# Head of a two-block attention kernel in another order, bias vectors moved into the MLP, and loop steps spread otherwise

## The chip, the cores and the metric

The kernel runs on one core of one Trainium2 chip. The metric is the device time of one execution in microseconds (us). All data are float32.

## The reference, cut to what matters

The input `x` has shape (2, 512, 32, 32). Two blocks follow each other.

```python
# block 0: deformable attention, 8 groups of 64 channels, 64 sampled keys per group
xn  = bn(x)
q   = gconv1x1(xn, qw)
off = tanh(einsum(gelu(depthwise6x6_stride4(q) + off_dw_b), off_pw_w)) * 4
vgrid = normalised(grid + off)                   # 64 key positions per group
kv  = bilinear_sample(xn, vgrid);  k, v = gconv1x1(kv, kw), gconv1x1(kv, vw)
pos = grid_q - vgrid                             # 1024 queries x 64 keys x 2
b   = sign(pos) * log1p(abs(pos))
b   = relu(b @ cpb_w1 + cpb_b1)                  # 2 -> 128
b   = relu(b @ cpb_w2 + cpb_b2)                  # 128 -> 128
b   = b @ cpb_w3 + cpb_b3                        # 128 -> 1
x   = x + out_w @ (softmax(q k / 8 + b) v) + out_b
x   = x + mlp_w2 @ gelu(mlp_w1 @ bn(x) + mlp_b1) + mlp_b2
# block 1: full attention over the 1024 positions, 512 channels
q, k, v = x Wq' + bq, x Wk' + bk, x Wv' + bv
x = x + (softmax(q k' / sqrt(512)) v) Wp' + bp
```

The position bias is the heavy part: its 128-to-128 layer runs for 2 x 8 groups x 1024 queries x 64 keys.

## The kernel before, in words

**Head.** The kernel first computes what is needed before its main loop. `chain(0)` (L251) normalises one 128-channel tile of `x` (L260), projects it to `q` on TensorE (PE, L266) with four copies out of PSUM (L271), runs the 36 taps of the depthwise convolution on VectorE (DVE, L303 and L305), GELU, a small projection (`po`, L345), tanh, and the positions of the keys with `sign * log1p` (L365 to L390). It writes the result to a DRAM buffer `fdr` through four DMAs on the queue of SyncE (SP), L392. `rank` and `arrange` (L208, L227) sort the hidden channels of the bias network by the sign of the last weight and permute its weights (`cw2`, `sc`). `weights(0)` and `weights(1)` (L518) multiply pairs of 512x512 matrices of block 1 on PE (`psg`, L524): Wq with Wk, and Wv with Wp. `vectors` (L534) does the same for the biases bq and bv: matmuls `psu` (L539) and `put` (L548) and the vector `ub` of block 1.

Each of these is a Python generator. The order in the head is the order in which lines 560 to 579 advance them, and `tc.issue_after` pins some pieces behind a given instruction. Around these pins the Tile layer orders instructions itself, engine by engine; each engine then runs its own list strictly in order.

**Loop.** `NS` = 256 steps `s`, each for four keys of one group. `load_tables` broadcasts a slice of `fdr` to all partitions (L592), `st_tables` makes tables `ta` and `tb` for 16 keys, that is every fourth step (L602, L609). `st_layer1(s + 2)` adds them on DVE with a saturating add into `h1` (L621, three buffers), `st_layer2(s)` is 64 matmul records on PE (L638) with four evictions on ScalarE (ACT, L645 and L647), `st_sum` joins them on DVE (L655), two accumulating DMAs of GpSimd (POOL) and one DMA of SP fold them, and every fourth step `st_layer3` (L703) adds to the logits.

Two background generators are spread over the steps. `bg` is `later()` (L480): the chains 1 to 4 and `sample` (keys and values), one `yield` piece per step. In chain 1 (one 128-channel tile) and chains 2 to 4 (two tiles each) the convolution taps run on ACT (L313), `TAPS[ci]` taps per piece, and DVE reduces them (L328). `tails` holds `softmax_steps` (L711) of a finished group, one piece per step:

```python
            if tails:
                with tc.issue_after(evicted[s][s % 4 == 0]):
                    if next(tails[0], 0) is not None:
                        tails.pop(0)
```

**After the loop.** `project` (L878) multiplies the attention output by `out_w` as seven Strassen-like products (L884) for each image, taken by DVE (L892, L123) with three PSUM buffers; `normalise` (L922) and `spread` prepare the MLP. Eight units of the MLP (L937) and block 1 (L1056, L1154) follow. Weights come over SP's queue (`load_unit`, L861).

Of the kernel before, what the change touches and what calls it, by code (L numbers as in the profile page):

```python
# [14 lines left out]
P = 128  # L15
# [11 lines left out]
TAPS = [36, 12, 4, 3, 3]  # L27
# [7 lines left out]
    ("bq", 4), ("bv", 4), ("bp", 4), ("dwb", 1), ("cb1", 1), ("cb3", 1),  # L35
# [11 lines left out]
def conv_seq_kernel(ctx: ExitStack, tc: tile.TileContext, x, xt, kst, pst, cst, vec, wsm, outw, w1, w2, wl, out):  # L47
# [16 lines left out]
    for i, g in enumerate(("bn1g", "bn2g")):  # L64
        nc.gpsimd.tensor_scalar(
            bns[:, 4 * i : 4 * i + 4], vs[:, VOFF[g] : VOFF[g] + 4], INV_BN, None, ALU.mult
        )
# [73 lines left out]
    with tc.tile_pool(name="lp", bufs=2) as lp:  # L141
# [20 lines left out]
        nc.gpsimd.memset(prod, 0.0)  # L162
# [12 lines left out]
        nc.scalar.dma_start(out=pz[:, 0:413], in_=pst)  # L175
        nc.scalar.dma_start(out=ws[:, 1024:1408], in_=wsm[:, 1536:1920])
        nc.scalar.dma_start(out=ident, in_=kst)
        nc.scalar.dma_start(out=cs, in_=cst)
# [6 lines left out]
        xn0 = load(0, 0)  # L185
        nc.scalar.dma_start(out=ws[:, P:1024], in_=wsm[:, P:1024])
# [20 lines left out]
        perm, place = pw_[:, 256:384], pw_[:, 384:512]  # L207
        def rank():  # L208
            nc.gpsimd.memset(one, 1.0)
            nc.gpsimd.tensor_scalar(po_, wb[:, 0:1], 0.0, None, ALU.is_ge)  # L210
            ps = flat("rank")
            nc.tensor.matmul(ps[:, 0:1], tri, po_, start=True, stop=True)
            nc.tensor.matmul(ps[:, 512:513], one, po_, start=True, stop=True)
            nc.scalar.copy(rn, ps.rearrange("p (h n) -> p h n", h=2)[:, :, 0])
            r_, n_ = rn[:, 0:1], rn[:, 1:2]
            nc.gpsimd.tensor_scalar(pc, chan, n_, r_, ALU.add, ALU.subtract)
            nc.gpsimd.tensor_scalar(dc, pc, r_, po_, ALU.subtract, ALU.mult)
            nc.gpsimd.tensor_tensor(pc, pc, dc, ALU.subtract)
            nc.vector.tensor_scalar(k16, four, n_, 4.0, ALU.is_le, ALU.mult)
            nc.vector.tensor_reduce(t4, k16, AX.X, ALU.add)  # L220
            free, bound = ([t.rearrange("p (a b l) -> p b a l", a=2, b=2)[:, i] for t in (place, crow)] for i in (0, 1))
            nc.vector.tensor_scalar(bound[0], bound[1], t4, 64.0, ALU.is_ge, ALU.mult)
            nc.vector.tensor_tensor(bound[0], bound[0], bound[1], ALU.add)
            nc.vector.tensor_scalar(free[0], free[1], t4, None, ALU.add)
            nc.vector.tensor_scalar(perm, place, pc, None, ALU.is_equal)

        def arrange():  # L227
            ps = flat("perm")
            nc.tensor.matmul(ps[:, 0:P], w2t, perm, start=True, stop=True)
            for z in range(4):  # L230
                for u in range(4):
                    nc.tensor.matmul(
                        ps[32 * u : 32 * u + 32, 512 + 2 * z : 514 + 2 * z], perm[:, 32 * z : 32 * z + 32], wb,
                        start=True, stop=True,
                    )
            nc.scalar.copy(cw2, ps[:, 0:P])
            nc.scalar.copy(
                sc[:, 0:8].rearrange("p (a z) -> p z a", a=2), ps[:, 512:520].rearrange("p (z a) -> p z a", a=2)
# [7 lines left out]
            nc.gpsimd.tensor_scalar(w3u[:, 28:32], mask[:, 8:12], sc[:, 8:9], None, ALU.mult)  # L246

# [3 lines left out]
        def chain(ci):  # L251
# [3 lines left out]
            for i in range(K):  # L255
                k = k0 + i
                if i == 0:
                    xn = xn0 if ci == 0 else load(b, k)
                    yield
# [10 lines left out]
                for f_, h_, f, h in QUADS:  # L270
                    nc.scalar.copy(  # L271
                        qa[f_, b, k, h * 512 : (h + 1) * 512], ps[h_, f * 512 : (f + 1) * 512]
                    )
                if i + 1 < K:
                    xn = load(b, k + 1)
                yield
# [64 lines left out]
            ps = flat("po")  # L341
            with tc.issue_after(marks[0]) if ci == 0 else nullcontext():
                for i in range(3):
                    for f in range(2):
                        nc.tensor.matmul(  # L345
                            ps[:, f * 512 + i * n // 2 : f * 512 + (i + 1) * n // 2],
                            pw[i][64 * f : 64 * f + 64, :],
                            gof[64 * f : 64 * f + 64].rearrange("p k j -> p (k j)"), start=True, stop=True,
                        )
# [4 lines left out]
            for f in range(2):  # L354
                nc.scalar.activation(
                    th.rearrange("p i (f k) j -> p f i (k j)", f=2)[:, f],
                    ps[:, f * 512 : f * 512 + 3 * n // 2].rearrange("p (i m) -> p i m", i=3), AF.Tanh,
                )
            if ci == 0:

                nc.scalar.activation(hb[:, 9:10], thf[:, 3 * n - 1 : 3 * n], AF.Ln, bias=1.0, scale=0.0)
            if ci > 0:
                yield
            for i in range(3):
                nc.vector.scalar_tensor_tensor(  # L365
                    th[:, i], th[:, i], 4.0, jg[:, i].unsqueeze(1).to_broadcast([P, 2 * K, J]),
                    ALU.mult, ALU.add,
                )
            nc.vector.tensor_scalar(thf, thf, 2.0 / 7.0, -1.0, ALU.mult, ALU.add)
# [7 lines left out]
            if ci > 0:  # L377
                yield
            nc.vector.tensor_scalar(u, ab, 1.0, None, ALU.add)
# [5 lines left out]
            nc.vector.reciprocal(u, u)  # L385
            nc.vector.tensor_tensor(er, er, u, ALU.mult)
# [4 lines left out]
            for c in range(4):  # L391
                nc.sync.dma_start(  # L392
                    out=fdr[ci][:, c, :, :].rearrange("g p j -> p g j"),
                    in_=ab.rearrange("p (g c j) -> p g c j", c=4, j=KT)[:, :, c, :],
                )
# [111 lines left out]
        with tc.issue_after(nc.cur_bb.bb.instructions[-1]):  # L507
            nc.sync.dma_start(out=wv, in_=wsm[:, 1024:1536])
            nc.sync.dma_start(out=ow_s, in_=outw)
        gs = lp.tile([P, 2, NCH, C], F32, tag="h1", name="gs", bufs=3)  # L510
        bz = ph.tile([P, 2 * NCH, 32], F32, tag="xnt", name="bz")
        nc.gpsimd.memset(bz, 0.0)
        for i, bn in enumerate(("bq", "bv")):
            nc.gpsimd.tensor_copy(
                bz[:, i * NCH : (i + 1) * NCH, 0], vs[:, VOFF[bn] : VOFF[bn] + NCH]
            )

        def weights(i):  # L518
            ps = [flat("psg") for _ in range(2)]
            for o in range(NCH):  # L520
                if o == NCH - 1:
                    yield
                for k in range(NCH):
                    nc.tensor.matmul(  # L524
                        ps[k // 2][:, k % 2 * 512 : k % 2 * 512 + 512], wls[i][:, 0, o, k * P : (k + 1) * P],
                        wls[i][:, 1, o, :], start=(o == 0), stop=(o == NCH - 1),
                    )
            for k2 in range(2):
# [4 lines left out]

        def vectors():  # L534
            ps = flat("psu")
            rows = ph.tile([P, 2, C], F32, tag="wt", name="rows")
            for i in range(2):
                for o in range(NCH):
                    nc.tensor.matmul(  # L539
                        ps[32 * o : 32 * o + 32, 512 * i : 512 * i + 512], bz[:, i * NCH + o, :],  # L540
                        wls[i][:, 1, o, :], start=True, stop=True,
                    )
            nc.scalar.copy(rows.rearrange("p i c -> p (i c)"), ps)
            yield
            ps = flat("put")
            for i in range(2):
                for k in range(NCH):
                    nc.tensor.matmul(  # L548
                        ps[:, 512 * i + k : 512 * i + k + 1], rows[:, i, k * P : (k + 1) * P], ones,
                        start=True, stop=True,  # L550
                    )
            nc.scalar.copy(ub, ps.rearrange("p (i c) -> p i c", i=2)[:, :, 0:NCH])
            nc.gpsimd.tensor_tensor(
                ub[:, 1, :], ub[:, 1, :], vs[:, VOFF["bp"] : VOFF["bp"] + NCH], ALU.add
            )

        def newest(engine):
            return next(i for i in reversed(nc.cur_bb.bb.instructions) if i.engine == engine)

        marks = []  # L560
        head, g, n, v = chain(0), weights(0), weights(1), vectors()
        next(head)
        next(head)
        rank()
        next(head)
        next(g)
        marks.append(newest(mybir.EngineType.PE))
        next(head)

        with tc.issue_after(newest(mybir.EngineType.PE)):  # L570
            next(g, None)
        for _ in head:
            pass
        arrange()
        next(v)
        next(n)
        with tc.issue_after(newest(mybir.EngineType.PE)):
            next(v, None)
# [19 lines left out]
        def st_tables(c):  # L598
# [3 lines left out]
            nc.scalar.activation(  # L602
                ta.rearrange("p j x -> p x j"), fb[:, 0], AF.Identity, bias=col("cb1"), scale=col("w1x")
            )
# [167 lines left out]
        for s in range(NS):  # L772
# [37 lines left out]
            if tails:  # L810
# [28 lines left out]
    nc.gpsimd.tensor_tensor(uc, ub[:, 0, 0:2], ub[:, 0, 2:4], ALU.add)  # L839
# [16 lines left out]
    with ExitStack() as top, tc.tile_pool(name="wp", bufs=2) as wp:  # L856
# [171 lines left out]
        for i, (b, p) in enumerate(units):  # L1028
            if 0 < i < len(units) - 1:
# [6 lines left out]
            layer1(p, wa, xb, hm)  # L1036
            if p == NU - 1 and b == 0:
# [4 lines left out]
            if p == NU - 1 and b == 0:  # L1042
                spread([xb[:, j] for j in range(7)])

# [212 lines left out]
def _layout(np, inputs):  # L1257
# [7 lines left out]
    def twice(v):  # L1265
# [6 lines left out]
        "mb2": cols(L0["mlp_b2"]), "bq": cols(L1["bq"]), "bv": cols(L1["bv"]), "bp": cols(L1["bp"]),  # L1272
# [29 lines left out]
    def quarters(w):  # L1302
# [15 lines left out]
        "wl": wl,  # L1318
    }
# [20 lines left out]
```

## Time and profile before

| What | Value |
|---|---|
| Times of three runs | 2689.32, 2689.59, 2691.59 us (median 2689.59) |
| Profiled execution | 2690.77 us, span of its instructions 2688.9 us |
| Granted clock of TensorE | 0.998 |
| Busy in the span | PE 2664.8 us (99%), DVE 2244.6 (83%), ACT 1689.0 (63%), POOL 575.3 (21%) |
| First L638 matmul (loop begins) | 46.60 us |
| First L937 matmul (MLP begins) | 1996.00 us |

"Busy" is the share of the span in which an engine ran an instruction. A row of the timeline has the start, the length, the engine, the line, the operation with its tiles, and in brackets how long the engine sat idle before it and what it waited for. PEld is the weight load of PE, which overlaps its matmuls; SPq and POOLq are the queues that issue DMAs.

### The profile page before, as it was taken

What the parts mean: (1) busy time and instruction counts of PE and PEld (TensorE: products, weight loads), DVE (VectorE), ACT (ScalarE), POOL (GpSimd) and SP (SyncE); (2) the same over time, 40 slices, a digit from 0 to 9 for tenths busy, and PEclk for the clock granted to TensorE, in tenths of its full rate; (3) what the DMA queues carried; (4) which work ended last, traced back from release to release, by engine and by line L of the source; (5) the groups of instructions that cost most, each with busy time, mean ns of one, the idle gap of its engine ahead of it and who ended that gap; (6) DMA issues with size and microseconds to landing.
All of it is one profiled execution on the core that took longest, in us unless ns stands there. A gap on an engine that the chain in (4) does not pass through costs nothing.

```text
span 2688.9 us, 46981 instructions
## 1 busy us (share of the span) xinstructions
PE 2664.8 (99%) x19628; PEld 955.2 (36%) x19628; DVE 2244.6 (83%) x1337; ACT 1689.0 (63%) x2191; POOL 575.3 (21%) x617
## 2 busy tenths in 40 slices
PE   9999999999999999999999999999999999999999
PEld 3323323232333323233333333333344444446455
DVE  5999999999999999999999999999765484466354
ACT  4787798789878788877777777777621131114041
POOL 1222222222222222222222222222243222000000
PEclk9999999999999999999999999999999999999999
DMA  5667776677666676666676776766631110000000
GB/s 186 146 147 148 154 148 138 139 159 154 141 148 144 150 149 145 139 147 142 148 155 138 148 151 145 147 149 142 134 122 47 47 47 32 16 16 0 31 1 31
DMA packets 95219, 314.05 MB, mean 117 GB/s; under 512 B 17184, under 2 KB 19872, under 8 KB 92320
## 3 DMA queue, kind: packets, MB, share of 16 engines
q0 software_dynamic: 57168, 201.88, 40.4%
q1 hardware_dynamic: 36832, 108.02, 11.2%
q8 instruction: 155, 2.54, 0.4%
q10 hardware_dynamic: 1008, 1.15, 0.1%
q14 instruction: 56, 0.46, 0.0%
HBM read 71.67 MB, written 6.55 MB: 29 GB/s over the span
## 4 chain that ended last, share of the span: by engine, by line
PE 85%; DVE 6%; issue 4%; ACT 2%; DMA 2%; SPq 0%; POOL 0%; DVEq 0%; POOLq 0%; ACTq 0%
PE ps L638 54%; PE sw L937 14%; PE sw L1056 9%; DVE h L621 3%; PE sw L1154 2%; PE sim L703 2%; PE psg L524 1%; PE sw L884 1%; DVE ub L655 1%; DMA ua<-uo 1%; DVE uo L655 1%; DMA ua<-ua 0%; ACT prod L313 0%; DVE ua L655 0%; ACT rx L645 0%
## 5 line engine op out<-in xcount | busy, mean ns | idle before, releaser
L638 PE MATMUL ps<-h,cw 128*32 128x512 f32 x16384 | 1786.6, 593 | 12.3 <-ACT rx L645 10.7
L621 DVE CUSTOM_DVE_ANT_1 h<-ta,tb 128x4096 f32<-128x4096 f32 (+1 forms) x257 | 1131.3, 4402 | 47.0 <-PE ps L638 42.0
L638 PEld LDWEIGHTS ps<-h,cw 128*32 128x32 f32 x16384 | 533.9, 110 | 1231.7 <-issue 1151.7
L645 ACT ACTIVATE rx<-ps,sc 128x1024 f32<-128x1024 f32 x512 | 568.3, 1110 | 175.0 <-PE ps L638 165.5
L647 ACT ACTIVATE ub<-ps,sc 128x1024 f32<-128x1024 f32 x256 | 308.0, 1203 | 96.4 <-PE ps L638 96.2
L655 DVE SCALAR_TENSOR_TENSOR ub<-rx,sc,ub 128x1024 f32<-128x1024 f32 x256 | 326.5, 1275 | 5.7 <-ACT ub L647 5.5
L657 POOL DMA_DIRECT2D ua<-ub x128 | 115.1, 899 | 723.6 <-DVE ub L655 692.3
L937 PE MATMUL sw<-xb,w1t 128*128 128x512 f32 x448 | 193.7, 592 | 1.3 <-DVE xs L123 1.3
L657 POOL DMA_DIRECT2D uo<-ub x127 | 119.3, 939 | 348.8 <-DVE ub L655 289.0
L937 PE MATMUL sw<-hm,w2t 128*128 128x512 f32 x448 | 193.6, 592 | 0.0
L647 ACT ACTIVATE ua<-ps,sc 128x1024 f32<-128x1024 f32 x128 | 154.1, 1204 | 58.5 <-PE ps L638 58.3
L674 POOL DMA_DIRECT2D ua<-uo x126 | 109.7, 870 | 365.2 <-DMA ua<-uo 355.5
L647 ACT ACTIVATE uo<-ps,sc 128x1024 f32<-128x1024 f32 x128 | 154.1, 1204 | 42.0 <-PE ps L638 38.8
L655 DVE SCALAR_TENSOR_TENSOR ua<-rx,sc,ua 128x1024 f32<-128x1024 f32 x128 | 163.5, 1277 | 12.5 <-ACT ua L647 12.5
L655 DVE SCALAR_TENSOR_TENSOR uo<-rx,sc,uo 128x1024 f32<-128x1024 f32 x128 | 163.5, 1277 | 11.8 <-ACT uo L647 11.8
L123 DVE TENSOR_TENSOR hm<-hm,sw 128x1024 f32<-128x1024 f32 x56 | 67.5, 1220 | 110.8 <-PE sw L937 110.6
L669 POOL DMA_DIRECT2D ua<-ua x126 | 154.8, 1229 | 2.6 <-DMA ua<-ub 1.5
L937 PEld LDWEIGHTS sw<-xb,w1t 128*128 128x128 f32 x448 | 85.1, 190 | 108.8 <-issue 105.0
L946 ACT ACTIVATE hm<-hm,vs 128x512 f32<-128x512 f32 x64 | 42.6, 714 | 129.0 <-DVE hm L123 129.0
L937 PEld LDWEIGHTS sw<-hm,w2t 128*128 128x128 f32 x448 | 85.2, 190 | 107.1 <-issue 106.4
L123 DVE TENSOR_TENSOR xs<-xs,sw 128x1024 f32<-128x1024 f32 (+1 forms) x48 | 55.5, 1170 | 72.2 <-PE sw L1056 36.0
L1056 PE MATMUL sw<-aT,vt 128*128 128x512 f32 x224 | 96.7, 593 | 0.3 <-ACT aT L1136 0.3
(237 smaller groups left out, 1798.7 us busy)
## 6 DMA issues: line engine op xcount, KB each, us to landing
ua<-ub POOLq DMA_DIRECT2D x128, 512.0 KB, 4.8
uo<-ub POOLq DMA_DIRECT2D x127, 512.0 KB, 5.4
fb<-fdr SPq DMA_DIRECT2D x64, 512.0 KB, 5.1
ua<-ua POOLq DMA_DIRECT2D x126, 256.0 KB, 6.4
ua<-uo SPq DMA_DIRECT2D x126, 256.0 KB, 2.8
ua<-uo POOLq DMA_DIRECT2D x126, 256.0 KB, 3.8
w1t<-in_w SPq DMA_DIRECT2D x8, 1024.0 KB, 4.8
w2t<-in_w SPq DMA_DIRECT2D x8, 1024.0 KB, 4.8
```

The lines of the kernel that those rows point to most:

```text
L123: nc.vector.tensor_tensor(out, a, b_, op)
L621: nc.vector._custom_dve(TENSOR_ADD_SAT, out=h1[:, y : y + step].rearrange("p y t x -> p (y t x)"), in0=a.unsqueeze(1).to_broadcast([P, ste ...
L638: nc.tensor.matmul(ps[32 * q : 32 * q + 32, h, :], cw2[:, 32 * z : 32 * z + 32], h1[:, 16 * h : 16 * h + 16, q, :], start=True, stop=True,)
L645: nc.scalar.activation(o, ps, AF.Relu, bias=sc[:, 4 + z : 5 + z])
L647: nc.scalar.activation(o, ps, AF.Relu, bias=sc[:, 4 + z : 5 + z], scale=sc[:, z : z + 1])
L655: nc.vector.scalar_tensor_tensor(r[1], r[0], sc[:, z : z + 1], r[1], ALU.mult, ALU.add)
L657: nc.gpsimd.dma_start(out=sums[s][1], in_=sums[s][3], accum_op=ALU.add)
L669: nc.gpsimd.dma_start(out=lanes(s, 0), in_=lanes(s, 1), accum_op=ALU.add)
L674: nc.gpsimd.dma_start(out=lanes(s, 1), in_=lanes(s + 1, 0), accum_op=ALU.add)
L703: nc.tensor.matmul(sims[gi][q : q + 32, :], w_, t[:, h, :], start=(i == 0 and f == 0), stop=(i == NSL // 4 - 1 and m == len(parts[e]) - 1),)
L937: nc.tensor.matmul(ps[:, m, :], w[:, a, k, m * P : (m + 1) * P], x[:, b_, k, :], start=(k == 0), stop=(k == 1),)
L1056: nc.tensor.matmul(ps[:, m, :], w[:, a, k, c + m * P : c + (m + 1) * P], x[b_][:, k, :], start=(k == 0), stop=(k == nk - 1),)
```

## The change

The change has four parts.

1. **Head.** `vectors` is dropped. The normalisation scales are computed on DVE, three loads move from ACT's queue to POOL's, the load of the later q and k weights moves to the end of SP's list. `rank`, `order` (split off from it) and `arrange` use small PSUM tiles of the pool `simp` and other places in the order: the first matmuls of `weights(0)` now come before `rank`. Half of the copies of chain 0 go to DVE. The Ln table is loaded without waiting for tanh, x and y of the keys are placed after the write to `fdr`, and `u = ab + 1` moves from DVE to ACT. The four writes of each chain to `fdr` become one. The first table is made in two pieces.
2. **Chain pieces.** `TAPS` of chain 1 goes from 12 to 6 taps per piece; two `yield`s per chain go away; the next chain's `x` tile is loaded when the previous one has been projected.
3. **Softmax pieces.** No softmax piece in steps with `s % 4 == 0`, but for the last 16 steps.
4. **Bias vectors in the MLP.** For each of the eight units, SP loads a 128x512 slice of weights (`wr`, one buffer) and DVE multiplies it by the broadcast bias row (`br`, one buffer) and sums along the row into `ub`. In the built program the eight DVE instructions (L1032 of the changed kernel) stand among the last ones of `project` and the first ones of the MLP.

```diff
-TAPS = [36, 12, 4, 3, 3]
+TAPS = [36, 6, 4, 3, 3]
...
     for i, g in enumerate(("bn1g", "bn2g")):
-        nc.gpsimd.tensor_scalar(
+        nc.vector.tensor_scalar(
...
-        nc.scalar.dma_start(out=pz[:, 0:413], in_=pst)
         nc.scalar.dma_start(out=ws[:, 1024:1408], in_=wsm[:, 1536:1920])
-        nc.scalar.dma_start(out=ident, in_=kst)
-        nc.scalar.dma_start(out=cs, in_=cst)
+        nc.gpsimd.dma_start(out=cs, in_=cst)
+        nc.gpsimd.dma_start(out=pz[:, 0:413], in_=pst)
+        nc.gpsimd.dma_start(out=ident, in_=kst)
...
-        nc.scalar.dma_start(out=ws[:, P:1024], in_=wsm[:, P:1024])
...
                 if i == 0:
-                    xn = xn0 if ci == 0 else load(b, k)
-                    yield
+                    xn = xn0.pop()
...
                 for f_, h_, f, h in QUADS:
-                    nc.scalar.copy(
-                        qa[f_, b, k, h * 512 : (h + 1) * 512], ps[h_, f * 512 : (f + 1) * 512]
-                    )
+                    copy = nc.vector.tensor_copy if ci == 0 and h == 1 else nc.scalar.copy
+                    copy(qa[f_, b, k, h * 512 : (h + 1) * 512], ps[h_, f * 512 : (f + 1) * 512])
...
-                nc.scalar.activation(hb[:, 9:10], thf[:, 3 * n - 1 : 3 * n], AF.Ln, bias=1.0, scale=0.0)
+                with tc.issue_after(newest(mybir.EngineType.Activation)):
+                    nc.scalar.activation(hb[:, 9:10], ones, AF.Ln)
...
+            place_keys(2 if ci == 0 else 0, 3)
...
             nc.scalar.activation(ab, pos, AF.Abs)
-            if ci > 0:
-                yield
-            nc.vector.tensor_scalar(u, ab, 1.0, None, ALU.add)
+            nc.scalar.activation(u, ab, AF.Identity, bias=1.0)
...
-            nc.vector.reciprocal(u, u)
-            nc.vector.tensor_tensor(er, er, u, ALU.mult)
+            rc = acc.rearrange("p a k y x -> p (a k y x)")[0:64, 0:n]
+            nc.vector.reciprocal(rc, u)
+            nc.vector.tensor_tensor(er, er, rc, ALU.mult)
...
-            for c in range(4):
-                nc.sync.dma_start(
-                    out=fdr[ci][:, c, :, :].rearrange("g p j -> p g j"),
-                    in_=ab.rearrange("p (g c j) -> p g c j", c=4, j=KT)[:, :, c, :],
-                )
+            nc.sync.dma_start(
+                out=fdr[ci].rearrange("g c p j -> p (g c) j"), in_=ab.rearrange("p (g j) -> p g j", j=KT)
+            )
+            if ci == 0:
+                place_keys(0, 2)
...
+            nc.sync.dma_start(out=ws[:, P:1024], in_=wsm[:, P:1024])
...
-        head, g, n, v = chain(0), weights(0), weights(1), vectors()
-        next(head)
-        next(head)
-        rank()
+        head, g, n = chain(0), weights(0), weights(1)
         next(head)
         next(g)
-        marks.append(newest(mybir.EngineType.PE))
+        with tc.issue_after(newest(PE)):
+            rank()
         next(head)
-
-        with tc.issue_after(newest(mybir.EngineType.PE)):
-            next(g, None)
+        with tc.issue_after(newest(PE)):
+            next(g)
+        marks.append(newest(PE))
+        next(head)
+        with tc.issue_after(newest(PE)):
+            next(g)
+        order()
         for _ in head:
             pass
-        arrange()
-        next(v)
-        next(n)
-        with tc.issue_after(newest(mybir.EngineType.PE)):
-            next(v, None)
+        with tc.issue_after(newest(mybir.EngineType.Activation)):
+            next(g, None)
+        with tc.issue_after(newest(PE)):
+            arrange()
+        with tc.issue_after(newest(PE)):
+            next(n)
         next(n, None)
...
-            if tails:
+            if tails and (s % 4 or s >= NS - NSL):
...
         for i, (b, p) in enumerate(units):
+
+            j, k = divmod(i, NCH)
+            if k == 0:
+                br = cp.tile([P, C], F32, tag="kz", name="br")
+                nc.sync.dma_start(out=br, in_=brow[j].partition_broadcast(P))
+            wr = f_pool.tile([P, C], F32, tag="ss", name="wr")
+            nc.sync.dma_start(out=wr, in_=wlt[:, i])
...
             layer1(p, wa, xb, hm)
+            nc.vector.scalar_tensor_tensor(
+                wr, wr, 1.0, br, ALU.mult, ALU.mult, accum_out=ub[:, j, k : k + 1]
+            )
```

## The prediction

> **What bounds the kernel now.** I read first the page's busy times and costliest groups:
>
> ```profile
> PE 2664.8 (99%) x19628; PEld 955.2 (36%) x19628; DVE 2244.6 (83%) x1337; ACT 1689.0 (63%) x2191; POOL 575.3 (21%) x617
> L638 PE MATMUL ps<-h,cw 128*32 128x512 f32 x16384 | 1786.6, 593 | 12.3 <-ACT rx L645 10.7
> ```
>
> PE is busy 99%. So only three things can change the time: PE work that goes or comes, PE's idle gaps (2688.9 - 2664.8 = 24.1 us), and time in which PE runs slowly. In the timeline I then looked where these lie. The start:
>
> ```profile
> 6.26 1.24 ACT L260 ACTIVATE xn<-xn,vs,bns 128x1024 f32<-128x1024 f32 x1 [3.60 <-DMA ws<-in_wsm]
> 10.17 0.59 PE L212 MATMUL rank<-pwork,pz 128*128 128x1 f32 x2 [1.53 <-POOL pwork L210]
> 12.89 0.34 PEld L524 LDWEIGHTS psg<-wl_s 128*128 128x128 f32 x1 [0.52 <-issue]
> 13.75 0.34 PEld L524 LDWEIGHTS psg<-wl_s 128*128 128x128 f32 x1 [0.52 <-issue]
> 17.57 0.19 PEld L524 LDWEIGHTS psg<-wl_s 128*128 128x128 f32 x1 [0.24 <-issue]
> 18.00 0.19 PEld L524 LDWEIGHTS psg<-wl_s 128*128 128x128 f32 x1 [0.24 <-issue]
> 29.04 1.92 PE L539 MATMUL psu<-wl_s,bz 128*32 128x512 f32 x16
> 41.29 1.84 PE L548 MATMUL put<-ones,rows 128*128 128x1 f32 x16
> 41.66 4.49 DVE L621 CUSTOM_DVE_ANT_1 h<-ta,tb 128x2048 f32<-128x2048 f32 x2 [0.81 <-ACT ta L602]
> 46.60 0.16 PEld L638 LDWEIGHTS ps<-h,cw 128*32 128x32 f32 x8 [0.76 <-ACT gs L529]
> ```
>
> Between 1.56 and 46.60 us PE is the chain. It waits for the first normalisation, then for `rank`, and the weight products `psg` start slowly: 0.86 us from record to record (12.89, 13.75) until 16.28, then 0.43 (17.57, 18.00). The first `h1` is whole at 41.66 + 4.49 = 46.15, 0.45 us before PE asks.
>
> In the loop a plain step takes 6.87 us (64 records at 0.43 us, four at a time). Larger gaps are few. Windows give PE's idle time: 1.4 us from 46.6 to 352, 4.8 from 352 to 506.5, 6.1 from there to 1940, 2.8 from 1940 to 1996. Those that the change touches:
>
> ```profile
> 153.85 3.60 ACT L313 ACTIVATE prod<-qa,vs 128x49 f32<-128x49 f32 x12
> 161.59 3.69 ACT L313 ACTIVATE prod<-qa,vs 128x56 f32<-128x56 f32 x12
> ...
> 493.04 6.00 SPq L392 DMA_DIRECT2D fdr<-fe  x4
> 506.47 1.07 PE L638 MATMUL ps<-h,cw 128*32 128x512 f32 x8 [3.00 <-ACT rx L645]
> 508.64 0.22 PEld L638 LDWEIGHTS ps<-h,cw 128*32 128x32 f32 x4 [0.64 <-issue]
> 509.50 0.22 PEld L638 LDWEIGHTS ps<-h,cw 128*32 128x32 f32 x4 [0.64 <-issue]
> ...
> 1972.09 2.34 DVE L123 TENSOR_TENSOR xs<-xs,sw 128x1024 f32<-128x1024 f32 x2
> 1975.21 1.23 DVE L111 TENSOR_TENSOR xb<-xb 128x1024 f32<-128x1024 f32 x1 [0.78 <-ACT xb L927]
> 1994.72 1.22 DVE L123 TENSOR_TENSOR xs<-xs,sw 128x1024 f32<-128x1024 f32 x1 [0.68 <-PE sw L884]
> 1996.00 24.30 PE L937 MATMUL sw<-xb,w1t 128*128 128x512 f32 x56 [1.31 <-DVE xs L123]
> ```
>
> Twelve taps at once (3.6 us) delay ACT's evictions at 157 and 165: 1.4 us of PE idle. Chain 2's table write holds SP for 6.00 us, so the next table lands at 503.6, ACT waits 4.1 us in front of its evictions, PE 3.0, and then runs four records at 0.85 instead of 0.43. From 1958 to 1996 DVE, not PE, sets the pace: `project` has three PSUM buffers, each freed by DVE, which idles 3 us there.
>
> **The head, step by step.** ACT's list loses three loads; `vs` has landed at 4.70 and `xn` at 4.5, so the normalisation starts at about 5.25 instead of 6.26, and the projection follows the warm-up matmuls at 6.55 without a gap. The first four `psg` matmuls (8 records) follow at once: their operands land at 5.3 and 6.5. PE was at full pace at 7.55 (the projection took 1.09 us) and became slow after the idle time from 8.64; with no idle time it stays fast. So: 7.5 + 8 x 0.43 = 10.95; `rank` 0.87 gives 11.8; nine more matmuls (18 records) 7.7: 19.5; `po` 0.81: 20.3; the last three 2.6: 23.0 with the change-over; `perm` 0.59: 23.6; `weights(1)` 32 records, 13.7: **37.3 us** instead of 46.6. In that, 3.7 us are the two bias stages (1.92 + 1.84), 2.6 us six slow records, the rest gaps and waits.
>
> The tables must keep up. GELU's input is ready by 17.7: DVE starts the taps at about 9.0 (copies shared, two of 0.58 us each) and needs 36 x 0.225 = 8.1 plus 0.6 for sums. Tanh ends at 21.0. Before, DVE waited 1.0 us for the Ln dummy, the logarithm waited for a copy, and the reciprocal for the logarithm: 25.58 to 31.82, 6.2 us. Now: five small DVE steps 1.2, Abs and add on ACT 0.9, then 0.94 + 4 x 0.3: ready at 25.3. The write landed at 37.0 before, behind the `xnt` load (36.8) and in the traffic of the `gdr` write (35.5); `xnt` is now loaded long before, `gdr` starts at 25.5. I take 4.5 us for the one write (median of the four 4.3), so 29.8; `fb` 3.3: 33.1; table 0.4; two halves of `h1` 4.5: whole at 38.1. PE needs the second half 0.86 after its start, at 38.2. Bounds: landing in 3.5 us (no effect) or in 6.5 (2 us later). I take a start of 37.8: **-8.8 us** (-6.5 to -9.3). Moving three loads to POOL costs three issues of about 0.85 (the row of `gdr`: 0.81), before POOL has other work; `rank` needs `pz` at 10.95, five us after issue at most 9: hidden, and a late `pz` would cost PE its own delay, 0 to 2.
>
> **The loop.** Six taps are 1.8 us, and 1.8 + 4.6 (four evictions) fits into 6.87: **-1.4** (0 to -1.8). With one `yield` less in front and three pieces more in chain 1, chain 2 writes at step 57 instead of 58, with its table due at 60 as before. So the write leaves about 7.5 us earlier, the table is not late, and the 3.0 us and four slow records (4 x 0.38) go: **-4.5** (0 to -4.7). What is late next: `sample` reuses the tile `fe` two steps behind the write, and ACT must wait until the write has been read. Before chain 4 this wait cost ACT 2.4 us at 1151 and PE 1.9. The merged write moves the same 64-byte rows (1024 of them; the four landed 6.8 us after the first issue at 1144.8). For chains 2 and 3 I add **+1.0** (0 to +4). Gaps at 359, 662 and 774 follow steps with tables, and softmax pieces leave such steps; but DVE is 100% busy in those windows (352 to 506: 152 of 154.5), so I count nothing: what ACT no longer delays, DVE does. At the end four softmax copies (1.05 us) now stand ahead of the last eviction, which had 0.28 us of slack: **+0.8**.
>
> **The bias in the MLP.** Eight DVE instructions on 128x512, taken as 0.7 us (the 0.74 of L892). `wr` has one buffer, so each load waits for the instruction before, and in the built order five stand in `project`, where the products that free PSUM queue behind them. A lone 256 KB load: 1 MB of `w2t` lands 5.0 us after its issue, of which 2.6 at the 400 GB/s seen in the head, leaving 2.4 + 0.65 = 3.1. The second instruction then ends at 77.85 (1977.85) where DVE went on at 75.21, less later waits for ACT; the third is covered by 11 us of other work; the fourth waits 0.6; the fifth waits for `br` and `wr` behind the fourth. Walked through, the last `xs` sum ends at 1999.2 instead of 1995.94: **+3.3** (+1.5 with 2.0 us loads, +9 with the 5.3 of the `xs` row). The three in the first MLP unit stand where DVE idles 2.2 us per product: nothing. The gap in front of the MLP grows to over 3 us, and the trace showed slow records after 3.0 (at 506) and not after 1.9 (at 1152): **+1.2** (0 to 1.7).
>
> The Trainium skill, "DMA: Bandwidth & Descriptors" ("Anatomy of one DMA - SWDGE (gpsimd) path"), fits about 2.0 us plus bytes over 436 KB/us, which for 256 KB is 2.6 us; with that figure, an estimate from the page, the term would be +1.9 instead of +3.3. The same page ("SWDGE vs HWDGE vs iDMA") gives POOL's path the slower setup, which speaks against moving three loads there; no row here shows these loads on POOL.
>
> **Sum.** -8.8 - 1.4 - 4.5 + 1.0 + 0.8 + 3.3 + 1.2 = -8.4. On the profiled execution's own 2690.77 that is 2682.4; it lies 1.2 above the median of 2689.59, from which the sum gives **2681.2 us**. About 0.2%, 5.4 us, is what a measurement of this kernel can tell from no change: faster is below 2684.2.
>
> **Rivals.** (a) *The loop gives nothing back*: DVE is the limit wherever ACT's stalls go, and the gap at 506 returns as a wait for `fe`. For it: DVE's 152 of 154.5 us. Against: at 503 DVE had `h1` ready some 4 us ahead. Then -8.8 + 1.0 + 0.8 + 4.5 = -2.5: 2687, no change. 18%. (b) *Slower: the serial `wr` loads hold DVE's queue in front of the MLP*. Three round trips (second, fourth, fifth) lie open. With landing time L the term is 3.3 + 3 (L - 3.1), and it must exceed 12.9 + 5.4 - 1.7 = 16.6 to make the kernel slower: L over 7.5 us. The longest 512 KB table load in the loop took 7.8, but the queues at 1974 are empty (no DMA traffic from 1963.5 on). At 8 us: +18, sum +6.8, 2696. With small errors elsewhere 14%. (c) *The head moves less because the tables, not PE, set the loop's start*: with the write as late as bounded, -6.5: 2683.5, still faster; part of my case.
>
> **Numbers.** My case and (c) 68%. All best bounds together give about -15 (2674); the range reaches up to rival (a) with two more bad bounds: 2674 to 2692. It leaves out (b) and a few per cent.
>
> **Right or wrong.** In the profile after: the first L627 record near 37.8 (wrong above 40); `psg` records 0.43 apart from the first; no PE gap of 3 us near 495; no twelve-tap group; DVE rows of L1032 that wait for `wr` 1 to 2.5 us in `project`; the first L925 matmul 6 to 10 us earlier than 1996.0. A wait for `wr` of 5 us or more, or a start of the loop after 42, would make the forecast wrong.

## The result, and the profile after

| | us |
|---|---|
| Before, median of ten runs | 2689.95 (2689.32 to 2691.97) |
| Changed, median of ten runs | 2683.65 (2681.93 to 2688.11) |
| Ratio, 95% interval | 0.9979 (0.9971 to 0.9987) |
| Profiled execution, time and span: before | 2690.77 and 2688.9 |
| Profiled execution, time and span: changed | 2688.11 and 2686.3 |

The change makes the kernel faster by 6.3 us in the medians, 0.21% by the ratio in the table; forecast were 8.4 us and 2681.2 us. The profile of the changed kernel happens to be that of its slowest run: it is only 2.6 us shorter than the one of before. Eleven later runs of the changed kernel gave a median of 2685.33 us; over all 21 it is 2684.45, and that figure the experiments below are set against. Where an experiment gives a ratio to the kernel before, that kernel was run beside it (median 2690.19 us in 15 runs for e1 to e4, 2690.86 in 21 runs for the others).

From the page of the changed kernel, the busy times and the costliest group:

```profile
PE 2663.3 (99%) x19596; PEld 960.0 (36%) x19596; DVE 2249.2 (84%) x1353; ACT 1688.3 (63%) x2193; POOL 576.9 (21%) x615
L627 PE MATMUL ps<-h,cw 128*32 128x512 f32 x16384 | 1789.6, 593 | 11.5 <-DVE kv L475 8.6
```

PE still waits little. But the last column has changed: before, 10.7 of 12.3 us of the waits of this group were put down to ACT's evictions (`rx`), now 8.6 of 11.5 us are put down to `kv`, four small DVE instructions of `sample` that no step of the forecast had priced.

The head, in selected rows of the changed kernel's timeline (start, length, engine, line, tiles, then the idle time before and its releaser):

```profile
7.75 3.70 PE L533 MATMUL psg<-wl_s 128*128 128x512 f32 x8
25.30 0.70 SPq L405 DMA_DIRECT2D fdr<-fe  x1
30.98 5.47 SPq L579 DMA_DIRECT2D fb<-fdr  x2
35.37 8.83 DVE L610 CUSTOM_DVE_ANT_1 h<-ta,tb 128x2048 f32<-128x2048 f32 x3 [0.23 <-ACT ta L590]
37.71 1.06 PE L627 MATMUL ps<-h,cw 128*32 128x512 f32 x8
39.91 5.36 PE L627 MATMUL ps<-h,cw 128*32 128x512 f32 x48 [1.14 <-DVE h L610]
```

`psg` is at full pace from its first record (eight in 3.70 us), and the loop starts at 37.71 instead of 46.60. The table's write was issued at 25.30 and the load of the table, which waits for it, at 30.98: 5.7 us. So the second half of the first `h1` is late and PE waits 1.14 us at 39.91.

The next table shows where the time lies. It is read from the traces of all kernels: the first matmul of step 0, of step 160 (by then the chains are done), of step 255 and of the MLP, and the end of the span. Kernels other than the first two are the experiments that follow.

| Kernel | loop starts | steps 0 to 160 | 160 to 255 | 255 to MLP | MLP to end |
|---|---|---|---|---|---|
| before | 46.60 | 1202.6 | 683.2 | 63.6 | 692.9 |
| changed | 37.71 | 1203.0 | 684.1 | 65.7 | 695.9 |
| a_changed_again | 37.26 | 1204.4 | 684.1 | 65.6 | 694.3 |
| e1_kv_first | 37.39 | 1191.4 | 684.1 | 66.5 | 694.6 |
| e2_no_bias | 37.54 | 1202.0 | 684.1 | 63.6 | 693.0 |
| e3_loop_as_before | 42.99 | 1201.2 | 683.3 | 65.6 | 694.8 |
| e4_late_bias | 37.69 | 1201.7 | 684.1 | 63.2 | 692.9 |
| e7_kv_bias_copies | 37.24 | 1191.5 | 684.1 | 64.0 | 693.0 |
| e8_and_softmax_as_before | 37.52 | 1193.9 | 683.7 | 63.8 | 693.0 |
| b1_before_kv_first | 47.10 | 1199.0 | 683.2 | 63.0 | 692.9 |

The head gives 8.9 us. The loop gives nothing back: 1885.8 us from step 0 to step 255 before, 1887.1 after. Then 2.1 us are lost in front of the MLP and 3.0 behind its start. -8.9 + 1.3 + 2.1 + 3.0 = -2.5.

Gaps of PE are given from here on as the distance from one record's start to the next beyond the usual 0.43 us. That is 0.16 us more than the idle time in brackets, because the profile shows a record as 0.59 us long. Their places are the starts of the last record before them.

In the loop the gaps of before that the change was forecast to remove are gone: 0.83 and 0.93 at 157 and 165 (twelve taps), 3.16 and four slow groups of four records at 503 (late table). So is 2.10 at 1152 (ACT's wait for `fe`), which no term of the forecast took away. New ones stand at 533 (2.42 us), 840 (2.93) and 1147 (3.76), each in a chain's first `sample` piece with matmuls. Selected rows of the changed kernel's timeline around the third:

```profile
1141.35 1.15 PE L462 MATMUL pkv<-wt,xnt 128*64 128x64 f32 x32
...
1143.60 1.28 DVE L644 SCALAR_TENSOR_TENSOR ub<-rx,sc,ub 128x1024 f32<-128x1024 f32 x1
1144.80 1.28 DVE L644 SCALAR_TENSOR_TENSOR uo<-rx,sc,uo 128x1024 f32<-128x1024 f32 x1
1146.00 0.25 DVE L735 RECIPROCAL sm<-sm 128x16 f32<-128x16 f32 x1
1146.16 4.36 DVE L610 CUSTOM_DVE_ANT_1 h<-ta,tb 128x4096 f32<-128x4096 f32 x1
1150.55 0.84 DVE L475 SCALAR_TENSOR_TENSOR kv<-pkv,bns,sg 64x32 f32<-64x32 f32 x4
1151.54 6.26 PE L627 MATMUL ps<-h,cw 128*32 128x512 f32 x32 [3.59 <-DVE kv L475]
```

The `pkv` matmuls (1141.35) fill one of the three PSUM buffers that the loop's matmuls also use. The buffer comes free when DVE has run `kv`. In DVE's list `kv` stands behind the `h1` of the next step; DVE is late here: that `h1` starts 4.8 us after the matmuls, where in the samples without a gap it starts 0.1 to 1.0 us after them. So `kv` starts at 9.2 us. PE has gone through the other buffers by 5.4 us and waits. That figure holds for all sixteen samples of the two traces: `kv` 7.0, 7.8, 8.3 and 9.2 us after its matmuls goes with gaps of 1.57 (before, at 874), 2.42, 2.93 and 3.76 us, each time 5.4 us less; one at 5.7 goes with 0.26, and the others, at 5.5 us or earlier, with less than 0.1.

In front of the MLP the timeline shows the bias products and their waits (selected rows):

```profile
1965.32 0.68 DVE L1032 SCALAR_TENSOR_TENSOR wr<-wr,br 128x512 f32<-128x512 f32 x1
1968.73 0.69 DVE L1032 SCALAR_TENSOR_TENSOR wr<-wr,br 128x512 f32<-128x512 f32 x1 [1.59 <-DMA wr<-in_wlt]
1979.92 0.68 DVE L1032 SCALAR_TENSOR_TENSOR wr<-wr,br 128x512 f32<-128x512 f32 x1
1983.36 0.69 DVE L1032 SCALAR_TENSOR_TENSOR wr<-wr,br 128x512 f32<-128x512 f32 x1
1988.57 0.69 DVE L1032 SCALAR_TENSOR_TENSOR wr<-wr,br 128x512 f32<-128x512 f32 x1 [0.72 <-DMA wr<-in_wlt]
1990.46 3.78 PE L925 MATMUL sw<-xb,w1t 128*128 128x512 f32 x4 [3.13 <-DVE xs L123]
```

Five products stand in `project`, the second waits 1.59 us for its load and the fifth 0.72, and PE waits 3.13 us instead of 1.31 before the first matmul of the MLP, whose first four records then take 3.78 us.

### The profile page after: what moved, and what is told of

It is laid out like the page before. It is cut to its first block, busy times and chain, and to the rows that moved or that the text cites. A ratio compares the mean times of both kernels' runs of the same rounds, so it can differ in the third digit from the quotient of the medians.

```text
span 2686.3 us, 46913 instructions
## 1 busy us (share of the span) xinstructions
PE 2663.3 (99%) x19596; PEld 960.0 (36%) x19596; DVE 2249.2 (84%) x1353; ACT 1688.3 (63%) x2193; POOL 576.9 (21%) x615
## 3 DMA queue, kind: packets, MB, share of 16 engines
q1 hardware_dynamic: 38176, 111.10, 11.6%
HBM read 74.28 MB, written 6.55 MB: 30 GB/s over the span
## 4 chain that ended last, share of the span: by engine, by line
PE 83%; DVE 6%; issue 5%; DMA 3%; ACT 2%; POOL 1%; DVEq 0%; SPq 0%; POOLq 0%; ACTq 0%
PE ps L627 52%; PE sw L925 14%; PE sw L1056 9%; DVE h L610 3%; PE sw L1154 2%; PE sim L692 2%; DMA ua<-ua 1%; DMA ua<-uo 1%; PE psg L533 1%; DVE ub L644 1%; PE sw L872 1%; DVE uo L644 1%; DVE ua L644 0%; ACT rx L634 0%; DMA wr<-in_wlt 0%
## 5 line engine op out<-in xcount | busy, mean ns | idle before, releaser
L627 PE MATMUL ps<-h,cw 128*32 128x512 f32 x16384 | 1789.6, 593 | 11.5 <-DVE kv L475 8.6
L627 PEld LDWEIGHTS ps<-h,cw 128*32 128x32 f32 x16384 | 541.2, 110 | 1225.0 <-issue 1155.7
L925 PE MATMUL sw<-xb,w1t 128*128 128x512 f32 x448 | 196.7, 600 | 3.1 <-DVE xs L123 3.1
L925 PE MATMUL sw<-hm,w2t 128*128 128x512 f32 x448 | 193.6, 592 | 0.0
L925 PEld LDWEIGHTS sw<-xb,w1t 128*128 128x128 f32 x448 | 86.1, 193 | 112.6 <-issue 106.4
L925 PEld LDWEIGHTS sw<-hm,w2t 128*128 128x128 f32 x448 | 85.1, 190 | 107.1 <-issue 106.7
```

The source lines that it names most:

```text
L627: nc.tensor.matmul(ps[32 * q : 32 * q + 32, h, :], cw2[:, 32 * z : 32 * z + 32], h1[:, 16 * h : 16 * h + 16, q, :], start=True, stop=True,)
L925: nc.tensor.matmul(ps[:, m, :], w[:, a, k, m * P : (m + 1) * P], x[:, b_, k, :], start=(k == 0), stop=(k == 1),)
```

## The experiments

**kv first.** Theory 1: the order in DVE's list makes the gaps. Theory 2: DVE has too much to do there, and any order gives them back.

```diff
+                state["kv"] = nc.cur_bb.bb.instructions[-1]
                 yield
...
             if s + 2 < NS:
-                st_layer1(s + 2)
+                kv_ = state.pop("kv", None)
+                with tc.issue_after(kv_) if kv_ is not None else nullcontext():
+                    st_layer1(s + 2)
```

> The changed kernel with one edit: the four kv instructions (L475) that empty the PSUM buffer of pkv stand in DVE's list ahead of the h1 (4.4 us) of the next step instead of behind it. Theory 1 (order): PE's three long gaps of the changed kernel (2.42 at 533, 2.93 at 840, 3.76 at 1147) are the time by which kv comes later than 5.4 us after its matmuls; kv now starts at most 4.5 us after them, these gaps go, and with them the slow records behind two of them (about 1.4 and 2.2). The loop from the first L627 to step 255 takes 1887.1 - 9 to 12.5 us, the time is 2672 to 2676. Theory 2 (amount of DVE work): DVE has no idle time in these stretches, so whatever is done first, the gaps return within 16 steps as waits for h1 or for kv; loop 1887 +- 2, time within 2 us of the changed kernel's 2683.7.

Measured: 2675.45 us (2672.94 to 2676.76), ratio to before 0.9942 (0.9929 to 0.9954). Steps 0 to 160 take 1191.4 us, 11.6 less than in the changed kernel's profile. The same sample in selected rows of this kernel's timeline:

```profile
1135.42 1.15 PE L462 MATMUL pkv<-wt,xnt 128*64 128x64 f32 x32
1138.40 7.05 PE L628 MATMUL ps<-h,cw 128*32 128x512 f32 x64
1140.07 0.84 DVE L475 SCALAR_TENSOR_TENSOR kv<-pkv,bns,sg 64x32 f32<-64x32 f32 x4
1142.15 4.42 DVE L611 CUSTOM_DVE_ANT_1 h<-ta,tb 128x4096 f32<-128x4096 f32 x1
```

`kv` now starts 4.6 us after its matmuls and `h1` follows; PE runs 64 records of the loop without a stop, and from 39 to 1091 us no gap of more than 0.6 us is left. On the page the group's waits fall from 11.5 to 3.7 us:

```profile
L628 PE MATMUL ps<-h,cw 128*32 128x512 f32 x16384 | 1785.4, 592 | 3.7 <-ACT uo L637 1.2
```

Theory 1 holds. Theory 2 is right in its premise only: DVE has no idle time from step 48 to 64 here either (0.00 us of 118.4). But that does not reach PE: `h1` has three buffers, and a late `h1` is covered by them where a late `kv` is not.

**The same edit in the kernel before.**

> The kernel before with one edit: kv ahead of h1 in DVE's list. Theory 1: there the gap of 3.0 us at 503 and those at 1144 to 1152 let DVE catch up ahead of the samples (kv 4.5 to 5.7 us behind its matmuls in seven of eight), so only the gap of 1.57 at 874 goes: 1 to 3 us below before. Then what the loop's parts of the change took away at 503 is real, and it is the place of kv that took it back. Rival: the place of kv is worth as much in any version, 8 us, and the loop's parts of the change are worth nothing with it or without it.

Measured: 2688.34 us (2685.06 to 2691.53) against 2690.86 of before (21 runs), ratio 0.9993 (0.9984 to 1.0002). Steps 0 to 160 take 3.6 us less, the gap at 874 is gone, that of 2.98 at 503 stays. So the order of `kv` costs the kernel before 2.5 us, which is not clear of noise (the interval reaches 1.0002), and the changed one 9.0 (2684.45 - 2675.45). By stage, from step 0 to 160, it is 3.6 and 11.6 us. With `kv` first, the changed loop is 7.6 us shorter from step 0 to 160 than the loop of before with the same edit (1191.4 against 1199.0); with `kv` behind, it is not shorter at all. What the change removed from the loop was real, and the place of `kv` took it back.

**The loop's parts taken back.**

```diff
-TAPS = [36, 6, 4, 3, 3]
+TAPS = [36, 12, 4, 3, 3]
...
                     xn = xn0.pop()
+                    yield
...
             nc.scalar.activation(ab, pos, AF.Abs)
+            if ci > 0:
+                yield
...
-            if tails and (s % 4 or s >= NS - NSL):
+            if tails:
```

and four writes for chains 1 to 4 as before.

> The changed kernel with the loop's parts of the change taken back: twelve taps in chain 1, softmax pieces in every step, the two yields of the chains back in place, four table writes for chains 1 to 4; the head and the bias in the MLP stay as changed. Theory 1 and 2 alike: the loop's parts gave nothing net, since chain 2's gap of 3 us for its late table is back (near 494) and lets DVE catch up, so kv comes without a long gap behind it; time within 2 us of the changed kernel's 2683.7. Rival (the forecast's sum): the loop's parts gave 4 to 5 us; time 2687.5 to 2689.

Measured: 2688.55 us (2685.75 to 2691.6), ratio to before 0.9992 (0.9983 to 1.0001). The time alone would speak for the rival, but the edit did more than intended: the first `yield` also stands in chain 0, whose pieces then fell into other places of the head, and the loop starts at 42.99 instead of about 37.5. By stage the loop takes 1201.2 + 683.3 = 1884.5 us, the changed one 1885.8 to 1888.5 in four profiles (`changed`, `a_changed_again`, e2, e4). So the loop's parts gave nothing there, as theory 1 and 2 both had it. The 4.1 us lost in the medians lie in the head, which is over 5 us longer. The gap in front of chain 2's table is back, 2.2 us at 500.6, and with it goes what theory 1 said: `kv` comes 4.6 to 5.7 us behind its matmuls in all eight samples, and PE's gaps there are 0.3 us at most.

**The bias products, left out and moved.** In e2 the loads and L1032 are gone and `ub` is set to zero, so that kernel leaves the bias vectors of q and v out and only prices them. In e4 each product is pinned behind the last DVE instruction of its unit's `layer1`:

```diff
-            nc.vector.scalar_tensor_tensor(
-                wr, wr, 1.0, br, ALU.mult, ALU.mult, accum_out=ub[:, j, k : k + 1]
-            )
+            with tc.issue_after(newest(mybir.EngineType.DVE)):
+                nc.vector.scalar_tensor_tensor(
+                    wr, wr, 1.0, br, ALU.mult, ALU.mult, accum_out=ub[:, j, k : k + 1]
+                )
```

> The changed kernel without the eight bias products: no br and wr loads, no L1032; ub is set to zero, so the bias vectors of q and v are left out. It prices this part. Theory: the waits for wr in front of the MLP and the slow records behind the 3.3 us gap cost what the trace shows: the first L925 comes 3.5 to 4.5 us earlier against the last step of the loop (65.65 us from step 255 to it in the changed kernel), its first matmuls 0.43 us apart at once (2.5 us more); time 5 to 7 us below the changed kernel's, 2677 to 2679. Rival: DVE's idle time in project takes the products up and the slow records come from the gap that was there before; time within 1.5 us of the changed kernel's.

> The changed kernel with each bias product (L1032) placed behind the last DVE instruction of its unit's first layer, so that none stands in project. Theory: DVE idles about 2 us for each product of the MLP, eight instructions of 0.77 us lie in that; the waits for wr leave the path, and the time is that of the kernel without the products within 1 us: 4 to 7 us below the changed kernel's. Rival: the price moves into the MLP, where each instruction delays the freeing of a PSUM buffer: 0 to 3 us below the changed kernel's.

Measured: 2682.01 us (2680.76 to 2682.28) without the products, 2681.39 (2679.74 to 2682.23) with the products later. Against 2684.45 that is 2.4 and 3.1 us, less than expected of both. By stage more of it shows: from step 255 to the end of the span it takes 761.5 us in the changed kernel's profile, 759.9 in its second one, 756.7 without the products and 756.1 with the late ones (756.4 before). That is 3.2 to 5.4 us, where e2 had been expected to give 5 to 7: the MLP began 2.0 us earlier after step 255 and not 3.5 to 4.5, and its first eight records took 3.0 us less (3.54 and not 6.55). The gap and the first matmuls of the MLP in the late version's timeline:

```profile
1986.75 9.71 PE L925 MATMUL sw<-xb,w1t 128*128 128x512 f32 x22 [1.31 <-DVE xs L123]
```

The wait is 1.31 us, as in the kernel before, and 22 records go at 0.44 us each. The products themselves cost nothing where DVE has idle time; the rival of the late version (a price within the MLP) falls with 692.9 us from the MLP to the end, as before.

**The changed kernel once more.**

> The changed kernel as it is, once more, for a second profile: its first one was of an execution of 2688.1 us, 4.5 above its median. Theory: the places of the gaps are the same (38, 533, 840, 1147, and before the MLP) and what differs between executions is how many PE records behind them run slowly (0.85 instead of 0.43 us apart), since the kernel without the bias products, which has no gap of 3.3 us in front of the MLP, scatters by 1.5 us and this one by 6. Median 2683 to 2685; a profile near the median has a stage from the last step to the 8th MLP record at least 2 us shorter than the first profile's 65.65 + 6.55, or a loop shorter by as much. Rival: the first execution had a longer head or gaps of another length; then these stages agree within 0.5 us and the difference lies elsewhere.

Measured: 2685.33 us, 2681.4 to 2687.93 in eleven runs. Inconclusive on its own question, since the profile again fell on a long execution (2687.45 us). It has the same gaps at the same places; the MLP's first eight records take 4.93 us instead of 6.55, the loop up to step 160 takes 1.4 us more. What the 21 runs do show is that time and granted clock go together: the eleven shortest (2681.4 to 2684.45) have a mean clock of 0.999 (eight) or 0.998 (three), and the seven longest (2685.92 to 2688.11) 0.996 or 0.997. 0.002 of 2685 us is 5.4 us, which is of the size of the scatter (6.7 us).

**Three edits together, and the softmax pieces.** e7 has `kv` first, the late products, and the copies of `psq` in chain 0 split by `f` instead of `h`. e8 adds `if tails:` as in the kernel before.

```diff
-                    copy = nc.vector.tensor_copy if ci == 0 and h == 1 else nc.scalar.copy
+                    copy = nc.vector.tensor_copy if ci == 0 and f == 1 else nc.scalar.copy
```

> The changed kernel with three edits: kv ahead of h1 in DVE's list, the bias products behind the first layer's last DVE instruction, and the four copies of psq in the head split by bank (f = 0 on ACT, f = 1 on DVE) instead of by halves of both banks. Theory: the copies no longer wait for each other, the taps start at about 9.2 instead of 10.6, the first h1 is whole 1.3 us earlier and the stall of 1.3 at 38 goes; loop start unchanged at 37.4 to 37.7. With the traces' prices (kv: span 2673.9; bias: 5.0; copies: 1.3) the span is 2667.6, the time 2669.4 (2668 to 2671). Rival: the medians' prices hold (8.2, 2.3, and 1.0): 2672 (2671 to 2674).

> The same three edits and one more: softmax pieces in every step of the loop again, not left out of the steps with tables. Theory: steps 160 to 255 take 683.3 us as in the two kernels whose softmax steps are those of before, instead of 684.1, and the last eviction no longer has four softmax copies in front of it (0.5 us gap at 1933): 0.8 to 1.3 us below the kernel with three edits. Rival: in steps with tables the softmax pieces delay ACT's evictions, the gaps of 0.4 to 1.1 us that before showed at 359, 662, 774 come back, 0.5 to 2 us above it.

Measured: e7 2671.66 us (2670.7 to 2675.14), ratio to before 0.9935 (0.9922 to 0.9947), the best version: 12.8 us below the changed kernel. It lies with the rival, the medians' prices (2672), and the copies gave nothing: in the built order DVE's copies wait for ACT's last one (8.66 us, taps from 10.09 instead of 10.57), and the stall of 1.30 us at 38 is still there. e8 took 2673.77 us (2673.21 to 2674.23), 2.1 us more: 0.4 us are won from step 160 on, 2.4 are lost before, where gaps such as 1.24 at 349 and 0.7 at 407 are back. Here the rival was right. Leaving the steps with tables free of softmax pieces is worth about 2 us in the loop, which the forecast had put at nothing.

## Why the prediction was right, and where it was not

The sign, the size within 2.5 us and the range (2674 to 2692) held. By its own steps:

- **Head, -8.8.** Right: loop start 37.71, forecast 37.8; `psg` fast at once. The loads moved to POOL landed 6.1 to 6.3 us after their issue, where on ACT's queue before it had been 3.7 to 5.2, but `pz` was there at 8.89 and `rank` started at 11.29, right behind the first `psg` records. The write took 5.7 us and not 4.5, so 1.3 of the 8.9 us came back as the stall in step 0; net -7.6, within the bounds given.
- **Taps, -1.4, and chain 2's table, -4.5.** Both gaps went, 1.8 and 4.7 us. The wait for `fe` behind the write (+1.0) did not come: in the changed kernel no ACT instruction waits for it, and that of 2.4 us in front of chain 4 went too.
- **"What is late next".** This is the step that failed. The forecast asked it of ACT and of the tile `fe`, and took DVE's 152 of 154.5 us only as a reason for rival (a). What was late next was `kv`: the gap at 503 had also been the time in which DVE caught up, and without it DVE's `h1` came 3.3 to 4.8 us after the samples' matmuls. 9.1 us of gaps came in, and behind those at 840 and 1147 ten slow groups of four records (1.45 and 2.23 us); without the stall of 1.3 us counted with the head, the loop's net was 0 and not -4.9. Rival (a) had the amount (the loop gives nothing back, 18%) and the wrong form: not a lack of DVE time, as e1 shows, but one short instruction behind a long one while PE's buffer waited for it.
- **End of the loop, +0.8.** Nothing: 63.6 us from step 255 to the MLP in e2, with the copies ahead of the last eviction, and 63.6 before.
- **Waits for `wr`, +3.3, and slow records, +1.2.** Together +4.5, measured +5.1 and +3.4 in the two profiles. The waits were mis-sized upwards (2.0 us: the second product waited 1.59 us as forecast, the fifth 0.72 and not a whole round trip), the slow records downwards (3.0 and 1.4). Three of the 256 KB loads landed 2.59, 2.61 and 2.69 us after their issue, where the sum had taken 3.1. The prediction's estimate from the Trainium skill ("DMA: Bandwidth & Descriptors", "Anatomy of one DMA - SWDGE (gpsimd) path"), 2.6 us and +1.9, was nearer, though that fit is for DMAs issued from GpSimd and these loads were issued by SP.
- **Rival (b)** did not come near: in front of the MLP the longest wait for `wr` was 1.6 us (in its first unit 2.4). The longest table load that this rival quotes, 7.8 us, is that up to 480 us; later in the loop of before one took 8.3. Nothing turned on it.
- **The signs.** The last one missed narrowly: the first L925 record came 5.5 us earlier than 1996.0 (1990.46), 4.6 in the second profile, and not 6 to 10. The others were seen.

The sum of the parts in the first profile is -2.5 and not -8.4, which is rival (a)'s sum; the medians differ by 6.3, and by 5.5 in the later runs (2690.86 and 2685.33). That they still came within 2.5 us of the forecast is in part luck: the head's gain was right, the loop's was not. Which parts are smaller in the shorter executions is not shown, since both profiles of the changed kernel are of long ones; the clock, 0.999 against 0.997, suggests that it is slow records for the most part.

## What to carry to other kernels

When a gap goes away, ask which engine used it to catch up, and look at that engine's list at the next place where another engine waits for it: a buffer whose release stands behind a long instruction is worth more attention than the engine's busy share. An instruction that frees a shared PSUM buffer belongs in front of work that has buffers in reserve. And judge a change of a few tenths of a per cent by stages, against more than one profile, with the clock beside it: here the profile that came first was 4.5 us from the median.

## What the runs showed of the hardware

The slow records cost more than expected and differ from run to run. The windows of the changed kernel (columns: window, length, busy time and count of PE, PEld, DVE, ACT and POOL, then the granted clock, the share of DMA and its GB/s) behind the gap at 1147 and at the start of the MLP:

```profile
1151.50:1157.70 6.20, 6.16 (x32) 1.61 (x32) 2.41 (x2) 1.11 (x1) 1.78 (x2) 0.57 1.00 236
1990.40:1996.50 6.10, 6.04 (x7) 2.52 (x8) 0.00 (x1) 0.00 (x0) 2.72 (x3) 0.50 0.99 367
```

and the start of the MLP in e7, after a gap of 1.48 us:

```profile
1976.80:1983.00 6.20, 6.16 (x15) 2.81 (x16) 0.00 (x0) 2.30 (x2) 4.29 (x4) 1.00 0.99 367
```

At a granted clock of 0.50 PE does 7 records in the time of 15. Windows of 5 us behind every PE gap of over 1.0 us between steps, in all ten traces, give this:

| Gap of PE beyond the usual distance | clock below 1.00 in the 5 us behind it | clock there |
|---|---|---|
| 1.0 to 2.16 us | never | 1.00 |
| 2.20 to 2.98 us | after 2.20, 2.25, 2.91, 2.93, 2.94; not after 2.22, 2.42, 2.87, 2.98 | 0.66 to 0.71 |
| 3.09 to 3.76 us | nine times of nine | 0.50 to 0.72 |

What PE loses behind a gap can be summed from the granted clock, as the time that it was withheld. In the middle row that is nothing in four cases and 1.4 to 1.7 us in five; in the last row it is 1.4 to 3.1 us. The gaps of 533, 840, 1147 and 1987 of the changed kernel lie in and above that zone, which fits its scatter of 6.7 us; e7 and e8 have no gap above 1.6 us, and nine of their ten runs a mean clock of 1.0. That the gaps make the scatter is not shown: b1 scatters by 6.5 us, and its profile has one gap in the zone (2.98 us). The Trainium skill, "TensorE: Matmul & The Clock Gate" ("HAM oscillation — how this bites in real kernels"), warns of idle gaps of PE above about 3.4 us, and its section on the clock gate ("What's actually happening") tells of a window of that length that runs free of the kernel. The rows here agree in kind, and a window that runs free could make it chance whether a gap is followed by slow records, which no run here shows; but the zone begins at 2.2 us here, so in this kernel a gap of 2.2 to 3 us should be priced with an even chance of about 1.5 us more behind it.

The merged table write was not quicker than its parts: 5.0 us to landing in the median of five, 4.7 in the median of the twenty before. What it saved is SP's time: 0.64 us of issue, where the four of chain 2 had held the queue for 6.00.
